# A graph-attention kernel on one core: a half-block opening of its set-up, loads of A tied to their buffers' release, and chunk ends spread over three cycles

## The chip, the cores and the metric

The kernel runs on one core of a Trainium2 chip. A core has TensorE (PE; its weight loads are listed as PEld), VectorE (DVE), ScalarE (ACT), GpSimd (POOL) and SyncE (SP), each with an instruction queue of its own. Transfers are issued from the queues of SP, ACT and POOL. The metric is the device time of one execution in microseconds; the median of several runs counts.

## The reference

Two layers over 4096 nodes with 512 features. The adjacency A (4096 x 4096) holds zeros and ones.

```python
def layer0(X, A, W, a_self, a_neigh, b):           # 8 heads of 64
    feats = einsum('nf,hfo->hno', X, W)
    s_self = einsum('hno,ho->hn', feats, a_self)
    s_neigh = einsum('hno,ho->hn', feats, a_neigh)
    dense = s_self[:, :, None] + s_neigh[:, None, :]
    dense = where(dense > 0, dense, 0.2 * dense) * A[None]
    out = einsum('hij,hjo->hio', softmax(dense, -1), feats) + b[:, None, :]
    return relu(transpose(out, (1, 0, 2)).reshape(N, 512))

x = layernorm(x + layer0(x, adj, ...))
# layer 1: attention inside the graphs that ptr marks (32 of 128 nodes),
# with Wq, Wk, Wv, and scores to which adj is added twice
x = layernorm(x + layer1(x, adj, adj, ptr, ...))
```

## The kernel before

The kernel has a fast path (`adjacency_streamed_path`) and a general path that runs only where the inputs do not have the expected form. Everything below is the fast path. It has a set-up, four passes over A (one for each pair of heads) and layer 1, which is worked into the last passes.

**Order of the work.** TensorE runs its instructions in the order of the program text (`manual_schedule` for PE). On the other engines, and in the three queues that issue transfers, a planner orders the instructions at build time; `keep_in_program_order` pins an instruction to its place in the program. Each queue is worked off in its order: an instruction that waits holds everything behind it.

**Set-up** (the block that begins with the pools `setup1`, `setup2`). The rows of x are worked in eight blocks of four 128-row tiles. `load_rows(k)` fetches block k into `xtp`, which has four buffers, so that a tile of block k+1 can be fetched once the transposes of the same tile of block k are done. Block 0 is issued from SP, all others from ACT. `turn_rows(k)` transposes the sixteen 128x128 pieces of a block into PSUM (L650), and ScalarE copies them, 512 columns at a time, to `xT_f` (L653), adding up `xs` on the way. `features(k, u)` multiplies a tile with W (L722, 8 matmuls, each of which the profile shows as two passes). W has two more columns for each head, the products with a_self and a_neigh, which VectorE works out at the start (L634 and L635); a scored tile reads 264 columns, an unscored one 256. Tiles 0 to 2 of block 0 are not scored there: `first_scores` makes up for them (L746, 12 matmuls of 16 columns). Because of the layout, features 0 and 1 of a block read x tiles 0 and 1 only, and features 2 and 3 read tiles 2 and 3.

VectorE adds b to each result (L733), which also frees its PSUM buffer (`ps_fe`, two of them). `exponentials` works out the softmax factors, and `scaled_features` writes f (`fst`: L775 on ScalarE, L776 on VectorE) and g to DRAM from POOL (L789). For block 0 this comes after `first_scores`. The factors' rows go to `pu_d`.

At the start SP issues x's first block, the two attention vectors, b in two layouts; ACT issues W in four slices and then block 1 of x.

**Passes.** `main_pass(r)` goes through four chunks of 1024 columns of transposed A. In a chunk there are 32 tiles j; with `wide=8` (passes 0 to 2) a chunk is four cycles of eight tiles. In each cycle VectorE makes `q` from p_row, d and the A tile (L1386), ScalarE makes most of the `mark`s from q (L1395), and TensorE does `accf` (A tiles and f, L1406), `acc` (q and g, L1426) and every eight tiles `dens` (marks, L1441). Pass 0 also sums over A (`ae`, L1350), and it makes the A tiles: `load_adjacency` fetches four tiles of A as fp8 from POOL into one of three buffers (L581), `bring` transposes them in pairs (L1130), ScalarE expands them to `at` (L1134), and POOL stores them to `at_d` (L1135) for the later passes. In pass 0, `load_adjacency` is called by `bring` where a group of four tiles is first used; three calls stand in the set-up. f_s, g_s, p_row and u_row come through SP (L1367, L1371, L1331, L1334).

**Chunk ends.** When a chunk is summed, `sums_to_rows` works out `ys` on VectorE (L1180 reads accf and u_row, L1188 adds acc), copies dens (L1190) and, in pass 0, ae (L1195, into the one buffer named hst) on ScalarE, and returns the rest as a generator `pieces`. In pass 0 its steps are: an empty first one; counts n0 and z from ae (L1203 on TensorE, L1208 to L1233 on VectorE); denominators from dens (L1237, L1240 to L1253); the output rows hst (L1260, L1261) and their store hs_d from POOL (L1271). Each `yield` names its price, and `run_pieces(budget)`, called once in a cycle, takes steps until the credit is used up:

```python
state["credit"] += budget
while state["credit"] > 0.0 and (work or ends):
    queue = ends or work
    try:
        state["credit"] -= next(queue[0])
    except StopIteration:
        queue.pop(0)
if not (work or ends):
    state["credit"] = 0.0
```

Before, the budget is 0.75 * wide = 6 in all passes, and a step of pass 0 costs 0.75 * wide = 6, the last one 1.8. So the four steps take one cycle each of the next chunk. In pass 0 the call stands between acc and dens.

Of the kernel before, what the change touches and what calls it, by code (L numbers as in the profile page):

```python
# [19 lines left out]
P = 128  # L20
# [384 lines left out]
def adjacency_streamed_path(  # L405
# [159 lines left out]
    def sums_to_columns(dst, part):  # L565

        for m in range(FC):
            nc.tensor.matmul(
                dst[:, m : m + 1], part[:, ts(m, P)], pick_col, start=True, stop=True
            )  # L570

    ats = {}
    a_bs = {}
# [12 lines left out]
    with tc.tile_pool(name="setup1", bufs=1, side="right") as one, tc.tile_pool(  # L586
# [12 lines left out]

        def load_rows(k):  # L600
            xts[k] = []
            for u in range(4):
                xt = xtp.tile([P, F], F32, name="xt_f")
                queue = nc.scalar if k else nc.sync
                queue.dma_start(xt, x[ts(4 * k + u, P), :])
                xts[k].append(xt)

        load_rows(0)
        FW = FH + 2
        w_sb = one.tile([P, FC, H, FW], F32, name="w_sb_f")  # L610
        for c in range(FC):
            nc.scalar.dma_start(
                w_sb[:, c, :, :FH], W[:, ts(c, P), :].rearrange("h p o -> p h o")
            )
        a_b2 = staged.tile([P, PR, 2, 2, FP], F32R, name="fst").bitcast(F32)
        a_b2 = a_b2[:, :2].rearrange("p r u s n -> p (r u s n)").rearrange(
            "p (k h o) -> p k h o", k=2, h=H
        )
        for k, v in enumerate((a_self, a_neigh)):
            nc.sync.dma_start(  # L620
                a_b2[:, k].rearrange("p h o -> p (h o)"), broadcast_rows(v, P, H * FH)
            )
        b_row = one.tile([P, H * FH], F32, name="b_row")
        nc.sync.dma_start(b_row, broadcast_rows(b, P, H * FH))
        b_col = one.tile([P, PR], F32, name="b_col")
        nc.sync.dma_start(
            b_col,
            bass.AP(tensor=b.tensor, offset=b.offset, ap=[[1, P], [FP, PR]]),
        )
        load_rows(1)  # L630
        for c in range(FC):
            prod = qp.tile([P, C], F32, name="q").rearrange("p (k h o) -> p k h o", k=2, h=H)
            for k in range(2):
                nc.vector.tensor_mul(prod[:, k], w_sb[:, c, :, :FH], a_b2[:, k])  # L634
                nc.vector.tensor_reduce(w_sb[:, c, :, FH + k], prod[:, k], AX.X, OP.add)  # L635
        powers = one.tile([P, 5, H], F32, name="powers")
        for i, v in enumerate((ALPHA, 1.0, ALPHA - 1.0, 1.0 - ALPHA, -ALPHA)):
            nc.vector.memset(powers[:, i, :], v)
        xs = one.tile([P, FC, NB], F32, name="xs")

        def turn_rows(k):
            xT = xTs[k] = two.tile([P, FC, 4, P], F32, name="xT_f")
            pts = {}

            order = [(u, c) for u in range(4) for c in range(FC)]
            for u, c in order if k == 0 else sorted(order, key=lambda x: x[1]):
                if u == 0:
                    last = k == 0 and c == FC - 1
                    pts[c] = misc([P, 4, P]) if last else pss.tile([P, 4, P], F32, name="ps_set")
                nc.tensor.transpose(pts[c][:, u, :], xts[k][u][:, ts(c, P)], ident)  # L650
            for c in range(FC):
                pt = pts[c]
                nc.scalar.activation(  # L653
                    xT[:, c], pt, AF.Identity, accum_out=xs[:, c, k : k + 1]
                )
# [59 lines left out]
        def features(k, u):  # L715
            pf = psf.tile([P, 2, HB], F32, name="ps_fe")
            pf = pf[:, :, : H * FW // 2].rearrange("p q (h w) -> p q h w", w=FW)
            scored = k > 0 or u == 3
            cols = slice(0, FW if scored else FH)
            for c in range(FC):  # L720
                for q in range(2):
                    nc.tensor.matmul(  # L722
                        pf[:, q, :, cols],
                        tile_j(xTs[k][:, c].rearrange("p u n -> p (u n)"), u),
                        w_sb[:, c, 4 * q : 4 * q + 4, cols],
                        start=(c == 0),
                        stop=(c == FC - 1),
                    )
            if u % 2 == 0:
                sums[k, u // 2] = qp.tile([P, C], F32, name="q").rearrange(  # L730
                    "p (u h o) -> p u h o", u=2, h=H
                )
            nc.vector.tensor_add(  # L733
                sums[k, u // 2][:, u % 2].rearrange("p (q h) o -> p q h o", q=2),
                pf[:, :, :, :FH],
                b_row.rearrange("p (q h o) -> p q h o", q=2, h=H // 2),
            )
            if scored:
                exponentials(k, u, pf[:, :, :, FH:])

        def first_scores():

            ps = pss.tile([P, 4, H, 2], F32, name="ps_set")
            for u in range(3):
                for c in range(FC):
# [7 lines left out]
                    )  # L753
            for u in range(3):
                exponentials(0, u, ps[:, u].rearrange("p (q h) w -> p q h w", q=2))

        def scaled_features(k, u):
            j, v, i = 4 * k + u, u // 2, u % 2
            fb = sums[k, v][:, i]
            if i == 0:  # L760
# [14 lines left out]
            nc.scalar.activation(fst[:, :, i, 0, :], fr, AF.Copy, scale=-1.0)  # L775
            nc.vector.scalar_tensor_tensor(  # L776
                fst[:, :, i, 1, :],
# [4 lines left out]
                op1=OP.subtract,  # L782
            )
            if i:
                for dst, n, src in (
# [4 lines left out]

        turn_rows(0)
        for k in range(NB):
            for u in range(4):
                features(k, u)
                if u == (0 if k else 2) and k + 1 < NB:
                    turn_rows(k + 1)
# [4 lines left out]
                if u == 2 and k:  # L801
                    columns_of_exponentials(k - 1)
                if u == 2 and k == 0:
                    first_scores()
# [311 lines left out]
    def bring(r, c, j):  # L1116
# [12 lines left out]
        for t in range(CT):  # L1129
            nc.tensor.transpose(pt[:, t, :], pairs[:, t, :], ident_b)  # L1130
        both = pt.rearrange("p t n -> p (t n)").bitcast(FP8).rearrange("p (n k) -> p n k", k=2)
        for k in range(2):
# [192 lines left out]
    def main_pass(r, ae=None, wide=4):  # L1325

        for c in range(NCH):
            p_row = []
            for h in range(2):
                p_row.append(rowp.tile([P, C], F32, name=f"p_row{h}"))  # L1330
                nc.sync.dma_start(p_row[h], broadcast_rows(pu_d[2 * r + h, ts(c, C)], P, C))  # L1331
            u_row = urowp.tile([P, C], F32, name="u_row")
            for h in range(2):
                nc.sync.dma_start(  # L1334
                    u_row[h * FH : (h + 1) * FH, :],
                    broadcast_rows(pu_d[H + 2 * r + h, ts(c, C)], FH, C),
                )
            def pieces(c, group, place):
                if r == PR - 1 and c:
                    run_plan(PLANS[c == NCH - 1][group][place])  # L1340
                elif place == (r == 0):
                    run_pieces(0.75 * wide)

# [17 lines left out]
            for j0 in range(0, NT, wide):  # L1361
# [3 lines left out]
                for k in range(j0 // 4, (j0 + wide) // 4):  # L1365
                    f_s[k] = fsp.tile([P, 4, 2, FP], F32R, name="f_s")
                    nc.sync.dma_start(  # L1367
                        f_s[k].rearrange("p u s n -> p (u s n)").bitcast(F32), f_d[r, k]
                    )
                    g_s[k] = gfp.tile([P, 4, 2, FH], F32, name="g_s")  # L1370
                    nc.sync.dma_start(g_s[k].rearrange("p u h o -> p (u h o)"), g_d[r, k])  # L1371
                if at_step == 0:
# [178 lines left out]
```

## Time and profile before

| what | value |
|---|---|
| median of 3 runs | 2066.62 us (2066.22 to 2067.95) |
| the profiled execution, its own time | 2068.04 us |
| its span, first to last instruction | 2066.2 us |
| set-up, from the first feature matmul to pass 0 | 13.93 to 165.16 us, TensorE busy 146.68 |
| pass 0 | 165.16 to 592.31 us, TensorE busy 423.32, VectorE 350.15, ScalarE 368.72 |
| passes 1 to 3 with layer 1 | 592.31 to 2066.2 us, TensorE busy 1456.69 of 1473.89 |

The profile is one execution. A row of a timeline gives start and duration in microseconds, the engine, the line of the program, the operation, what it writes and reads, and in brackets how long the engine had been idle and what ended that. ACTq, SPq and POOLq rows are the issues of transfers. In a row of windows each engine has its busy time, then follow the granted TensorE clock (1.00 is full speed), the mean busy share of the transfer engines and GB/s.

### The profile page before, as it was taken

Reading aid. Unit: us, or ns where it says so; the run is one execution under the profiler, and the core shown is the slowest. Engines: PE = TensorE matmul, PEld = TensorE weight load, DVE = VectorE, ACT = ScalarE, POOL = GpSimd, SP = SyncE. Lnnn points to the kernel's source line nnn. Section 1 sums busy time; section 2 is a strip of 40 time slices with the busy share of each in tenths; the row PEclk is TensorE's granted clock in tenths of the full one; section 3 lists DMA queues with packets and bytes.
Section 4 is the critical chain, followed back from the end, with each engine's and each line's share of the span. In section 5 each row is a group of like instructions: output and inputs, shape, how many; then the busy total and the mean of one; then the engine's idle time right before and its main releaser. Section 6 shows DMA issues by size and latency. Waiting matters only on the chain.

```text
span 2066.2 us, 38253 instructions
## 1 busy us (share of the span) xinstructions
PE 2030.9 (98%) x15086; PEld 1049.8 (51%) x15086; DVE 1670.1 (81%) x2125; ACT 1540.4 (75%) x1869; POOL 222.9 (11%) x361
## 2 busy tenths in 40 slices
PE   8999999999999999999999999999999999999997
PEld 6885555444445444444445444444454445445443
DVE  5667888888799998798999899998975884896654
ACT  3338888888878899788899899998885666567420
POOL 1223222222100000000000000000210210210111
PEclk9999999999999999999999999999999999999999
DMA  6989999999899999798999899989974773684211
GB/s 195 303 270 248 270 294 263 296 260 297 264 341 335 367 347 350 258 312 293 327 308 338 300 354 329 329 287 360 315 247 150 240 262 128 229 275 167 74 49 43
DMA packets 207371, 551.31 MB, mean 267 GB/s; under 512 B 24780, under 2 KB 65740, under 8 KB 207180
## 3 DMA queue, kind: packets, MB, share of 16 engines
q1 hardware_dynamic: 136716, 418.45, 58.1%
q0 software_dynamic: 62272, 121.91, 23.1%
q10 hardware_dynamic: 8192, 8.39, 1.2%
q8 instruction: 121, 1.98, 0.4%
q14 instruction: 70, 0.57, 0.1%
HBM read 491.79 MB, written 107.22 MB: 290 GB/s over the span
## 4 chain that ended last, share of the span: by engine, by line
PE 84%; DMA 7%; issue 4%; DVE 2%; ACT 1%; POOL 1%; POOLq 0%; ACTq 0%; DVEq 0%; SPq 0%
PE acc L1426 36%; PE accf L1406 20%; PE ps_m L1067 5%; PE ps_fe L722 5%; PE ps_m L995 5%; DMA at_d<-at 5%; PE dens L1441 5%; PE ps_m L1022 1%; DVE q L1386 1%; PE ps_m L1081 1%; DMA xt_f<-in_x_dram 1%; ACT mark L1395 1%; PE ps_m L975 1%; PE ps_m L1130 1%; PE ps_m L924 1%
## 5 line engine op out<-in xcount | busy, mean ns | idle before, releaser
L1386 DVE SCALAR_TENSOR_TENSOR q<-p_row,d_all,at 128x1024 f32<-128x1024 f32 x1024 | 1241.9, 1277 | 159.9 <-PE acc L1426 129.3
L1395 ACT ACTIVATE mark<-q,nb_all 128x1024 fp8e4<-128x1024 f32 x896 | 995.5, 1145 | 181.4 <-DVE q L1386 165.8
L1426 PE MATMUL acc<-q,g_s 128*32 128x512 f32 x8192 | 904.2, 593 | 1.4 <-DVE q L1386 0.4
L1426 PEld LDWEIGHTS acc<-q,g_s 128*32 128x32 f32 x8192 | 264.3, 110 | 595.3 <-issue 533.6
L1406 PE MATMUL accf<-at,f_s 128*128 128x512 f32 x2048 | 496.7, 398 | 1.9 <-issue 1.8
L1406 PEld LDWEIGHTS accf<-at,f_s 128*128 128x128 f32 x2048 | 380.5, 189 | 111.4 <-issue 28.1
L1151 ACT ACTIVATE ck<-ck,neg_half_f 128x1024 f32<-128x1024 f32 x128 | 146.0, 1141 | 21.7 <-DMA ck<-in_adj_dram 21.7
L1152 ACT ACTIVATE ck<-ck,neg_quarter 128x1024 f32<-128x1024 f32 x128 | 146.4, 1143 | 1.7
L1441 PE MATMUL dens<-mark,e_b 128*6 128x512 fp8e4 x2048 | 125.9, 379 | 0.9 <-ACT mark L1395 0.9
L722 PE MATMUL ps_fe<-w_sb_f,xT_f 128*128 128x264 f32 (+1 forms) x512 | 121.3, 394 | 4.6 <-ACT xT_f L653 4.6
L1134 ACT CAST at<-ps_m 128x1024 fp32r<-128x1024 fp8e4 x128 | 120.1, 1026 | 5.5 <-ACT mark L1395 3.0
L1067 PE MATMUL ps_m<-wvT,x1T 128*128 128x512 f32 x256 | 114.2, 594 | 0.0
L995 PE MATMUL ps_m<-x1T,M_sb 128*128 128x512 f32 x256 | 112.9, 595 | 0.0
L722 PEld LDWEIGHTS ps_fe<-w_sb_f,xT_f 128*128 128x128 f32 x512 | 100.7, 200 | 19.1 <-ACT xT_f L653 5.0
L1271 POOL DMA_DIRECT2D hs_d<-hst x12 | 10.7, 893 | 834.4 <-DVE hst L1261 816.1
L1391 DVE TENSOR_SCALAR mark<-q,d_all 128x1024 fp8e4<-128x1024 f32 x128 | 95.7, 748 | 4.8
L1441 PEld LDWEIGHTS <-e_b 128*6 128x6 bf16 x2048 | 55.8, 86 | 78.5 <-issue 36.2
L1135 POOL DMA_DIRECT2D at_d<-at x128 | 69.0, 539 | 178.0 <-ACT at L1134 107.4
L995 PEld LDWEIGHTS ps_m<-x1T,M_sb 128*128 128x128 f32 x256 | 48.0, 190 | 59.3 <-issue 58.4
L1067 PEld LDWEIGHTS ps_m<-wvT,x1T 128*128 128x128 f32 x256 | 47.6, 190 | 56.4 <-issue 55.1
L1075 DVE TENSOR_TENSOR v_t<-ps_m,bv_row 128x512 f32<-128x512 f32 x32 | 21.7, 683 | 60.5 <-PE ps_m L1067 60.5
L1002 ACT ACTIVATE zT<-ps_m,zb 128x512 f32<-128x512 f32 x32 | 21.8, 680 | 61.1 <-PE ps_m L995 61.1
(185 smaller groups left out, 1084.2 us busy)
## 6 DMA issues: line engine op xcount, KB each, us to landing
at<-at_d SPq DMA_DIRECT2D x384, 512.0 KB, 6.0
f_s<-f_d SPq DMA_DIRECT2D x128, 512.0 KB, 7.5
at_d<-at POOLq DMA_DIRECT2D x128, 512.0 KB, 14.9
ck<-in_adj_dram SPq DMA_DIRECT2D x128, 512.0 KB, 5.4
g_s<-g_d SPq DMA_DIRECT2D x128, 256.0 KB, 5.7
f_d<-fst POOLq DMA_DIRECT2D x16, 1024.0 KB, 7.2
a_b<-in_adj_dram POOLq DMA_DIRECT2D x32, 512.0 KB, 16.3
p_row<-pu_d SPq DMA_DIRECT2D x32, 512.0 KB, 6.7
```

Source lines behind the costliest of these rows:

```text
L722: nc.tensor.matmul(pf[:, q, :, cols], tile_j(xTs[k][:, c].rearrange("p u n -> p (u n)"), u), w_sb[:, c, 4 * q : 4 * q + 4, cols], start=(c ...
L995: nc.tensor.matmul(pz, L1["M"][:, f, ts(c, P)], x1T[:, f, :], start=(f == 0), stop=(f == FC - 1),)
L1067: nc.tensor.matmul(pv, x1T[:, f, ts(u, P)], L1["wvT"][:, f, :], start=(f == 0), stop=(f == FC - 1),)
L1134: nc.scalar.copy(at, both[:, :, k])
L1151: tc.keep_in_program_order(nc.scalar.activation(ck, ck, AF.Square, bias=neg_half))
L1152: nc.scalar.activation(ck, ck, AF.Abs, bias=neg_quarter, accum_out=binp[:, k : k + 1])
L1386: nc.vector.scalar_tensor_tensor(q, p_row[h], d_j, ats[r, c, j].bitcast(F32), op0=OP.max, op1=OP.mult)
L1391: nc.vector.tensor_scalar(mark, q, d_j, None, op0=OP.is_gt, saturate=False)
L1395: nc.scalar.activation(mark, q, AF.Sigmoid, bias=nb_all[:, j, hh : hh + 1], scale=BIG, saturate=False,)
L1406: nc.tensor.matmul(accf[:, s, :], f_s[j // 4][:, j % 4, w, :], ats[r, c, j][:, ts(s, HB)], start=(j == 0 and w == 0), stop=(j == NT - 1 an ...
L1426: nc.tensor.matmul(acc[o : o + 32, s, :], g_s[j // 4][:, j % 4, h, o % FH : o % FH + 32], qs[j, h][:, ts(s, HB)], start=(j == 0), stop=(j ...
L1441: nc.tensor.matmul(dens[lo : lo + 6, :], e_b[:, j, 2 * r + h, :], marks[j, h][:, ts(s, HB)], start=(j == 0), stop=(j == NT - 1),)
```

## The change

Set-up: block 0 of x is worked in two halves. SP now issues all loads of x and half of W, in a new order: x tiles 0 and 1, W slices 2 and 3, the two vectors (in two buffers), x tiles 2 and 3, b, and then the other blocks; ACT issues W slices 0 and 1 only and then runs a one-column activation. TensorE first does transposes of the identity, whose result nobody reads, then tiles 0 and 1; tiles 2 and 3 are transposed in the middle of features(0, 1), into the same PSUM tiles. All four tiles of block 0 are now scored by `first_scores`, and block 1 is transposed after features(0, 3) instead of after features(0, 2). The score columns of W slices 2 and 3 are worked out on VectorE after features(0, 0) and features(0, 1).

Loads of A: in pass 0, right after the transposes that read a buffer for the last time (j % 4 == 2), the load that reuses this buffer is issued, pinned, for the tiles 12 after the buffer's own first one.

Chunk ends: the budget of pass 0 is 1.0 * wide = 8; the prices stay.

Some loads of the first chunks of pass 0 on SP, and one VectorE instruction of block 0, are pinned to the program order.

```diff
+    def in_order(pinned, ins):
+        if pinned:
+            tc.keep_in_program_order(ins)
...
-        def load_rows(k):
-            xts[k] = []
-            for u in range(4):
+        def load_rows(k, us=range(4)):
+            xts.setdefault(k, [])
+            for u in us:
                 xt = xtp.tile([P, F], F32, name="xt_f")
-                queue = nc.scalar if k else nc.sync
-                queue.dma_start(xt, x[ts(4 * k + u, P), :])
+                nc.sync.dma_start(xt, x[ts(4 * k + u, P), :])
                 xts[k].append(xt)
-        load_rows(0)
+        load_rows(0, (0, 1))
...
         for c in range(FC):
-            nc.scalar.dma_start(
+            queue = nc.scalar if c < FC // 2 else nc.sync
+            queue.dma_start(
                 w_sb[:, c, :, :FH], W[:, ts(c, P), :].rearrange("h p o -> p h o")
             )
+        nc.scalar.activation(neg_quarter, neg_quarter, AF.Identity)
...
         for k, v in enumerate((a_self, a_neigh)):
+            nc.sync.dma_start(a_s[k], broadcast_rows(v, P, H * FH))
+        load_rows(0, (2, 3))
         b_row = one.tile([P, H * FH], F32, name="b_row")
         nc.sync.dma_start(b_row, broadcast_rows(b, P, H * FH))
+        load_rows(1)
...
+        def turn_rows(k, us=range(4)):
+            if us[0] == 0:
+                xTs[k] = two.tile([P, FC, 4, P], F32, name="xT_f")
+                turned.clear()
...
+            def keep_warm(n):
+                pw = psf.tile([P, 2, HB], F32, name="ps_fe")
+                for i in range(n):
+                    nc.tensor.transpose(pw[:, 0, :P], ident, ident)
+
+            order = [(u, c) for u in us for c in range(FC)]
             for u, c in order if k == 0 else sorted(order, key=lambda x: x[1]):
+                if (k, c) == (0, 0) and u < 2:
+                    keep_warm((9, 2)[u])
+                nc.tensor.transpose(turned[c][:, u, :], xts[k][u][:, ts(c, P)], ident)
...
-            scored = k > 0 or u == 3
+            scored = k > 0
...
+                if (k, u, c) == (0, 1, 1):
+                    turn_rows(0, (2, 3))
...
-            for u in range(3):
+            for u in range(4):
...
-        turn_rows(0)
+        turn_rows(0, (0, 1))
         for k in range(NB):
             for u in range(4):
                 features(k, u)
-                if u == (0 if k else 2) and k + 1 < NB:
+                if k == 0 and u < 2:
+                    score_columns(FC // 2 + u)
+                if u == (0 if k else 3) and k + 1 < NB:
                     turn_rows(k + 1)
...
-                if u == 2 and k == 0:
+                if u == 3 and k == 0:
                     first_scores()
...
         for t in range(CT):
             nc.tensor.transpose(pt[:, t, :], pairs[:, t, :], ident_b)
+        ahead = c * NT + j + 10
+        if j % 4 == 2 and ahead < NCH * NT :
+            tc.keep_in_program_order(load_adjacency(ahead // NT, ahead % NT))
...
                 elif place == (r == 0):
-                    run_pieces(0.75 * wide)
+                    run_pieces((0.75 if r else 1.0) * wide)
```

Where the diff is cut, it has the pins of SP's loads (p_row and u_row of the first two chunks of pass 0, f_s and g_s of its first two cycles), `score_columns`, which holds the former loop body of the score products, and the narrower evacuation in `turn_rows`, which sums block 0's second half into a ninth column of `xs`.

## The prediction

> **What bounds the kernel now.** I read the page's engine rows first, then the waits of TensorE in the first 640 us, then the engines' timelines where those waits lie. Row 1 of the page says that TensorE is the bound: 2030.9 of 2066.2 us. So only TensorE's idle time, a slower TensorE clock, or TensorE work that appears or goes can move the time; a wait on another engine counts where TensorE runs into it.
>
> ```profile
> PE 2030.9 (98%) x15086; PEld 1049.8 (51%) x15086; DVE 1670.1 (81%) x2125; ACT 1540.4 (75%) x1869; POOL 222.9 (11%) x361
> ```
>
> TensorE's waits up to 640 us (total, times, longest):
>
> ```profile
> PE ps_set L650 <- DMA xt_f<-in_x_dram: 6.4, 4, 3.9
> PE ps_fe L722 <- ACT xT_f L653: 4.6, 1, 4.6
> PE ps_m L1130 <- ACT at L1134: 2.0, 2, 1.2
> PE accf L1406 <- issue: 1.8, 1, 1.8
> PE ps_set L695 <- ACT pu_j L671: 1.3, 1, 1.3
> PE ps_m L1130 <- DVE hst L1214: 1.0, 3, 0.4
> PE dens L1441 <- ACT mark L1395: 0.9, 2, 0.7
> ```
>
> These seven are all in that stretch. A wait on loads of A (a_b) is not among them.
>
> The opening, on ScalarE, TensorE and TensorE again:
>
> ```profile
> 7.39 4.47 ACTq L605 DMA_DIRECT2D xt_f<-in_x_dram  x4
> 11.89 1.28 ACT L653 ACT_TABLE_LOAD   x1 [11.89 <-DMA w_sb_f<-in_L_gnn_W_dram]
> 13.19 0.60 ACT L653 ACTIVATE xT_f<-ps_set 128x512 f32<-128x512 f32 x1
> ...
> 13.93 12.03 PE L722 MATMUL ps_fe<-w_sb_f,xT_f 128*128 128x256 f32 x48 [4.61 <-ACT xT_f L653]
> ...
> 92.68 1.76 PE L650 MATMUL ps_set<-ident_f,xt_f 128*128 128x128 f32 x13 [1.24 <-DMA xt_f<-in_x_dram]
> ```
>
> ScalarE stands in its own DMA issues until 11.89 (the second block of x waits there for its buffers), then loads its table, and only then evacuates transposes that were complete at 9.3. Features start at 13.93. Block 5's x is late once more, at 92.
>
> The chunk ends, in the first pass's windows (one 8-tile cycle each; span, then busy PE, PEld, DVE, ACT) and timelines:
>
> ```profile
> 271.13:296.92 25.79, 25.79 (x245) 13.14 (x242) 21.77 (x20) 23.18 (x25) 6.07 (x10) 1.00 1.12 278
> 377.38:404.41 27.03, 26.37 (x244) 13.08 (x242) 24.23 (x22) 21.59 (x23) 6.09 (x10) 1.00 1.11 296
> ...
> 387.62 0.59 ACT L1195 COPY hst<-ae 128x512 f32<-128x512 f32 x1 [4.41 <-DMA hs_d<-hst]
> ...
> 590.93 1.27 DVE L1180 SCALAR_TENSOR_TENSOR ys<-accf,S_col,u_row 128x1024 f32<-128x1024 f32 x1
> ...
> 592.31 7.59 PE L1406 MATMUL accf<-at,f_s 128*128 128x512 f32 x32 [1.76 <-issue]
> ```
>
> Both windows are the first cycle of a chunk. In the first, no earlier result occupies hst; in the second, ScalarE's copy of ae waits 4.4 us for the store of the hst written one cycle before, marks come late, and TensorE pays. The last two lines are the step from pass 0 to 1: accf is released only when VectorE has done ys, behind two hst products of 1.28 us together; the row names "issue", but TensorE starts 0.1 us after ys ends.
>
> **The opening.** It removes ScalarE's x issues and half of its W issues, and loads its table early (issues to about 1.8, table 1.28: ready near 3.3). The first two tiles of x landed 3.0 and 4.5 us after issues at 0.73 and 1.15, so at 3.7 and 5.65; they stay first on SP. Four transposes took 1.1 us, so x1's end at 6.75, with the half-width evacuations beside them (half of 0.6 plus 0.2 each). W's second slice landed at 7.5 (issue 1.2, 6.3 us); its first precedes it. I take 6.8 for the first feature matmul, bounds 6.3 and 8.
>
> From there on TensorE: 264-column passes run 3.73 us for 16, 0.233 each, so 256 columns 0.226. Tiles 0 to 3 are 64 passes (14.5 us), the second eight transposes 1.0, the next sixteen 2.0, first_scores 32 passes at 3.13/24 = 0.13 (4.2), features(1,0) 3.7. Sum 25.4: block 2's transposes at 32.2 if the clock were full. Against before this order holds 16 score columns' matmuls instead of 12 (+1.0) and brings the second half's transposes onto the path (+1.0).
>
> The clock is not full. The granted clock shows no record before 17, but the first transposes took 421 ns and later ones 273, so the opening was slow: 12.03 us against 48 x 0.226 = 10.85. The one-microsecond windows show 0.50 from 30.7 to 34.1, after first_scores, and there 32 passes took 8.91 instead of 7.46. I charge the new start 1.6, and first_scores, longer now and with transposes just before it, 1.5 to 3.0. Transposes of block 2 then start at 35.3 to 36.8, before at 39.47: **3.4 us gained**, bounds 1 and 6.
>
> The change also adds eleven transposes of the identity, before x arrives and while x1 is awaited (9 x 0.27 = 2.4 us from 1.4: no delay). The Trainium skill, TensorE: Matmul & The Clock Gate, Part 4, speaks against them: transposes do not count as activity for the clock. The rows agree as far as they go (8 transposes between 7.3 and 9.3 raised nothing), but never show eleven in a row. By the rule the 1.6 stay; without it they go. Yet the third tile can't profit: its transposed rows wait on ScalarE behind fst, which needs VectorE's first add. That add follows four score products and four reductions (0.65 each) and a 0.22 cast from a_self's landing, which I put at 9.0 to 9.6 (now 9.0): add at 14.9 to 15.6, fst 0.63, evacuation 0.4, so 16.6. TensorE gets there at 16.7 by the slow sum. So a fast clock is worth at most some tenths here, and I take the rule.
>
> W's last slices move to SP and x's second half behind the vectors. The skill's Trainium Kernel Development and Optimization, Key Constraints, says that queues share the same DMA engines and only issue time is saved: by it I count no earlier bytes from two queues, only ScalarE's 11.89. The trace moved 262 GB/s over the first 13.93 us; ten transfers of 256 KB ahead of b_row put x2 and x3 at about 11, needed at 13.8.
>
> **Loads of x on SP.** They are issued as TensorE frees each buffer, with ScalarE's evacuations and issue gaps no longer between (block 5: transposes end 75.9, issues 76.5 to 77.9, landing up to 14.7). The early loads of f_s, g_s, p_row and u_row now stand behind them; they are needed at 160 and follow near 110. Block 5's delay goes: its transposes to features took 3.33 (90.95 to 94.28) against 1.87 elsewhere, **1.5 us**. Bounds 0 and 1.5. Block 2's x is the nearest to a new wait: issues 25 to 26.5, 5.3 us landing as at 29, needed at 35: 3 us spare.
>
> **Loads of A.** Now pinned on POOL right behind the transposes that free a buffer. TensorE waits for none before, and POOL waited for TensorE 23 times before such a load, so most already leave at the release; the first ones leave 4 to 15 us sooner. Worth 0. If it were harmful: at 0.85 to 1.05 DMA share after 163 these loads delay f_s of the second cycle, issued 171.5 to 175.5, needed 193.75, usually 7.5 in flight: 10 us of cover.
>
> **Chunk ends.** The budget per cycle rises from 6 to 8 while the price of a piece stays 6, so the empty first yield and the n0 piece both fall in the first cycle, the dens piece in the second, the output in the third. The same TensorE instructions: chunk 1's four windows are 25.79, 27.03, 26.50, 26.93, of which 25.8 is the plain cycle. What goes is what chunks 2 and 3 have above chunk 1: 27.03 + 27.42 + 26.49 + 26.94 = 107.88 against 106.25, and 26.19 + 27.39 + 26.53 = 80.11 against 79.32: **2.4 us**, since hs_d (10.5 us to land) now has a whole cycle before ae is copied. The short n0 wait (0.33 each, three times) moves and stays. At the pass step the hst products have gone a cycle earlier, and the changed program's order on VectorE puts ys ahead of the last eight q of the chunk: the 1.76 become about 0.2: **1.6 us**. Bounds of both: 1.5 and 4.2. VectorE has 3.9 us per cycle to spare, and n0's reductions are 2.1.
>
> **Sum:** 3.4 + 1.5 + 0 + 2.4 + 1.6 = 8.9. Behind the first cycles of pass 1 the instruction order is the old one and TensorE 99% busy, so it carries through. The profiled run took 2068.0 for a span of 2066.2; its sum gives a span of 2057.3 and 2059.1 outside. It lay 1.4 above the median of the runs, so the median becomes 2066.6 - 8.9 = **2057.7**.
>
> **Rivals.**
> *The opening gives almost nothing.* Two more slow windows of 3.4 us cost 1.7 each, or W or a_self lands 3 us late. For it: first_scores has already throttled the clock once; before pass 0 it was 0.50 for 10 us. Against: matmul stretches on both sides. Then 8.9 - 3.4 = 5.5: 2061.
> *More.* The clock windows fall well (their phase against the work is not fixed) and pass 0's slow start, 9.99 us for 32 accf passes that later take 7.6, loses less: 8.9 + 3 to 4: 2054.
> *Moved waits.* The opening gives 1 and n0 in the first cycle meets the late marks, keeping the 2.4: 1.5 + 1.6 + 1 = 4.1: 2062.5, within what can be told from nothing.
> *Slower: u_row holds SP at the pass step.* The changed order puts pass 1's u_row ahead of f_s on SP; it waits for ys, which releases the old one. If ys ran at 590.9 as now, f_s would leave at 592.2 instead of 575.9 and land 7.5 later; TensorE, ready at 590.5, would start near 602 instead of 592.3: 9.7 lost, 7.3 gained elsewhere, 2069. It decides once ys ends later than about 582. Against: ys only needs accf, complete at 572.9.
>
> **Numbers.** The forecast's case has 0.56, opening lost 0.20, more 0.12, moved waits 0.08, slower 0.04. A measurement here tells about 0.2%, 4.1 us, from no change. The forecast, "more" and most of the lost opening (0.17) are beyond that: faster 0.85, the same 0.11, slower 0.04. The range 2053.5 to 2063 reaches from "more" to the lost opening.
>
> **What would show it.** First feature matmul at 6.3 to 8; block 2's transposes at 35 to 37; no wait on xt_f after that; first cycles of chunks 2 and 3 alike at about 27; no 4 us wait before ae's copy; accf of pass 1 within 0.3 us of the last dens. I am wrong if SP holds u_row for ys, if the clock shows 0.50 in more windows, or if the second half of block 0 makes TensorE wait.

## The result and the profile after

The changed kernel takes **2056.78 us** (median of 6 runs, 2054.87 to 2059.1), the kernel before, run beside it, 2067.21 (6 runs, 2064.97 to 2070.18): ratio 0.9949, 95% interval 0.9936 to 0.9962, or 10.4 us less. The profiled run took 2055.59, with a span of 2053.8; the one before had 2066.2. Where these 12.4 us of span lie, by the start times of TensorE's instructions:

| stretch | before | after | difference |
|---|---|---|---|
| start to block 2's transposes (opening) | 39.47 | 33.65 | -5.8 |
| from there to pass 0's first accf | 125.69 | 124.11 | -1.6 |
| pass 0 | 427.15 | 423.56 | -3.6 |
| passes 1 and 2 | 772.29 | 772.42 | +0.1 |
| pass 3 and the rest | 701.6 | 700.1 | -1.5 |

The last row is not put down to the change: it is all in pass 3's seventh cycle (12.36 to 10.86), which lasted from 10.85 to 13.23 us in the thirteen profiles of this study with no relation to what was edited; its cause was not looked for.

TensorE's line of busy times in the page of the changed kernel, and its waits up to 640 us:

```profile
PE 2028.2 (99%) x15105; PEld 1051.6 (51%) x15105; DVE 1671.7 (81%) x2125; ACT 1540.6 (75%) x1878; POOL 226.6 (11%) x361
```

```profile
PE ps_m L1165 <- ACT at L1172: 2.4, 2, 1.6
PE accf L1454 <- DMA f_s<-f_d: 1.5, 1, 1.5
PE ps_fe L671 <- POOL ident_f masks.py:199: 1.4, 1, 1.4
PE ps_set L725 <- ACT pu_j L701: 1.3, 1, 1.3
PE ps_m L1165 <- DVE hst L1252: 1.0, 3, 0.4
PE ps_set L677 <- DMA xt_f<-in_x_dram: 0.5, 2, 0.3
PE ps_fe L752 <- ACT xT_f L680: 0.2, 1, 0.2
```

The 6.4 us for x and the 4.6 us for xT_f have shrunk to 0.5 and 0.2, and no dens waits for marks. New is the second row: accf waits 1.5 us for an f_s.

The opening on TensorE, in the changed kernel's timeline (start, length, line, what, count):

```profile
6.72 7.68 PE L752 MATMUL ps_fe<-w_sb_f,xT_f 128*128 128x256 f32 x24
...
17.23 7.18 PE L752 MATMUL ps_fe<-w_sb_f,xT_f 128*128 128x256 f32 x32 [0.22 <-ACT xT_f L680]
24.25 2.03 PE L677 MATMUL ps_set<-ident_f,xt_f 128*128 128x128 f32 x16
26.21 3.94 PE L778 MATMUL ps_set<-w_sb_f,xT_f 128*128 128x16 f32 x32
30.00 3.81 PE L752 MATMUL ps_fe<-w_sb_f,xT_f 128*128 128x264 f32 x16
33.65 2.09 PE L677 MATMUL ps_set<-ident_f,xt_f 128*128 128x128 f32 x16
```

Features start at 6.72 instead of 13.93, and the second half-block is met with a wait of only 0.22. The sixteen features after first_scores take 3.81: that is full speed. In the profile before, the granted clock was 0.50 at that place.

The same first cycles of chunks 1 and 2 as were shown of before, now in the changed kernel's windows (span; busy PE, PEld, DVE, ACT, POOL; granted clock; DMA share; GB/s), and below them the step into pass 1 in the timelines of SP, VectorE and TensorE, by time:

```profile
262.74:289.75 27.01, 26.67 (x248) 13.37 (x245) 22.99 (x28) 23.69 (x25) 6.67 (x10) 1.00 1.12 286
369.03:396.16 27.13, 26.78 (x248) 13.39 (x245) 23.39 (x28) 23.96 (x26) 6.18 (x10) 1.00 1.11 292
```

```profile
554.84 13.44 SPq L1155 DMA_DIRECT2D at<-at_d  x8
563.41 1.28 DVE L1218 SCALAR_TENSOR_TENSOR ys<-accf,S_col,u_row 128x1024 f32<-128x1024 f32 x1 [2.15 <-PE accf L1454]
568.38 1.09 SPq L1377 DMA_DIRECT2D u_row<-pu_d  x2
569.52 0.92 SPq L1411 DMA_DIRECT2D f_s<-f_d  x1
581.32 7.59 PE L1454 MATMUL accf<-at,f_s 128*128 128x512 f32 x32 [1.46 <-DMA f_s<-f_d]
```

Chunks 1 and 2 are alike, and ScalarE's copy of ae waits for no store. The first cycle of chunk 1 is 1.2 us longer, since it now holds a piece; the fourth cycles are 1.1 shorter. ys runs at 563.4, long before it is needed (before, it ran at 590.9, at the last moment). But f_s, which SP has put behind eight loads of at and two of u_row, is now the last to arrive.

### The profile page after: what moved, and what is told of

It is laid out like the page before. It is cut to its first block, busy times and chain, and to the rows that moved or that the text cites. A ratio compares the mean times of both kernels' runs of the same rounds, so it can differ in the third digit from the quotient of the medians.

```text
span 2053.8 us, 38310 instructions
## 1 busy us (share of the span) xinstructions
PE 2028.2 (99%) x15105; PEld 1051.6 (51%) x15105; DVE 1671.7 (81%) x2125; ACT 1540.6 (75%) x1878; POOL 226.6 (11%) x361
## 4 chain that ended last, share of the span: by engine, by line
PE 92%; DVE 4%; DMA 1%; issue 1%; SPq 0%; POOL 0%; ACT 0%; POOLq 0%; DVEq 0%
PE acc L1474 40%; PE accf L1454 23%; PE ps_m L1102 5%; PE ps_fe L752 5%; PE dens L1489 5%; PE ps_m L1030 5%; DVE q L1434 3%; PE ps_m L1165 1%; PE ps_m L1057 1%; PE ps_m L1116 1%; PE ps_m L1010 1%; PE ps_m L959 1%; PE ps_set L677 1%; PE ps_m L1298 1%; PE ae L1394 1%
```

## The experiments

All times are medians beside runs of the kernel before on the same chip, in three batches in which it took 2067.38, 2066.67 and 2067.31. A difference between two changed kernels goes across batches; by the intervals it is known to some 3 us. The change has three parts, and six kernels cover every combination of them beside the kernel before and the changed one (last row):

| set-up (opening, x on SP) | early chunk ends | rule for loads of A | us | before | ratio (95%) | difference by the ratio |
|---|---|---|---|---|---|---|
| new | - | - | 2065.87 | 2067.38 | 0.9994 (0.9985 to 1.0002) | -1.2 |
| - | new | - | 2064.24 | 2067.38 | 0.9985 (0.9978 to 0.9991) | -3.1 |
| - | - | new | 2077.20 | 2067.38 | 1.0040 (1.0027 to 1.0054) | +8.3 |
| new | new | - | 2062.46 | 2066.67 | 0.9979 (0.9971 to 0.9986) | -4.3 |
| - | new | new | 2064.00 | 2067.31 | 0.9984 (0.9977 to 0.9991) | -3.3 |
| new | - | new | 2073.86 | 2067.31 | 1.0034 (1.0024 to 1.0044) | +7.0 |
| new | new | new | 2056.78 | 2067.21 | 0.9949 (0.9936 to 0.9962) | -10.5 |

The single parts add up to +4.0; together they give -10.5. The rest of this section shows what lies between.

### One part alone: the set-up

```diff
-        ahead = c * NT + j + 10
-        if j % 4 == 2 and ahead < NCH * NT :
-            tc.keep_in_program_order(load_adjacency(ahead // NT, ahead % NT))
...
-                    run_pieces((0.75 if r else 1.0) * wide)
+                    run_pieces(0.75 * wide)
```

(from the changed kernel)

> The kernel before with the set-up of the changed kernel alone (half-block opening, x loads on SP, pinned order); loads of A and chunk ends as before. Theory (the set-up's gain reaches the end undiminished): in the changed kernel's trace the opening was 5.8 us and the rest of the set-up 1.6 us shorter, so the time is 7 to 8.5 us below before (ratio about 0.996), pass 0 starts at 157 to 159 us, and its cycles keep before's values of 27.0 and 26.2 in the chunk ends' third and fourth place. Rival A (the gain is partly the clock): the clock falls to 0.50 after the first scores as it did before, block 2's transposes start at 35 to 37 us, and the gain is 4 to 6 us. Rival B (pass 0 waits for its loads of A after all without the new rule): L1165's transposes or the at copies wait in the first cycles of pass 0, and 2 us or more of the set-up's gain are gone there.

The theory missed: -1.2 us, which the interval does not tell from nothing. What both rivals named is in the trace. The clock is at 0.50 for 6.8 us after first_scores (block 2's transposes at 37.3, a little past rival A's 35 to 37), pass 0 starts at 161.8 and is 430.98 long, 3.8 longer than before's. Its first cycle lasts 30.58 instead of 28.59, for TensorE waits 2.57 us for a load of A, and chunk 2's first cycle lasts 29.72 instead of 27.03: the copy of ae waits 7.1 us there for hs_d instead of 4.4.

### One part alone: the chunk ends

```diff
-                    run_pieces(0.75 * wide)
+                    run_pieces((0.75 if r else 1.0) * wide)
```

(from the kernel before)

> The kernel before with one number changed: pass 0's budget for chunk-end pieces is 1.0 x wide. Theory (what the changed kernel's trace shows): the two cycles that hold the late pieces get 1.5 and 0.8 us shorter in sum over chunks 1 to 3, and the step into pass 1 gains no more than 0.3 us, because the first f_s is now issued behind 8 loads of at and two of u_row: 2.6 us below before in all, ratio 0.9987. By the prediction's own sum 4.0 us (0.9981), with a wait of 0.2 us at the step. Rival (u_row's loads hold SP more where pass 0 starts later): the wait at the step is as long as before's 1.8 or longer and the gain 2 us or less.

Measured: -3.1 us (-4.5 to -1.9), which fits the theory's 2.6 and the prediction's own 4.0. In its profile pass 0 lasts 422.96, 4.2 less than before's, as in the prediction's sum. At the step there is no wait in this profile: f_s is issued 12.4 us after the last cycle's first accf, and accf of pass 1 starts 24.1 after it.

### One part alone: the rule for the loads of A

```diff
             nc.tensor.transpose(pt[:, t, :], pairs[:, t, :], ident_b)
+        ahead = c * NT + j + 10
+        if j % 4 == 2 and ahead < NCH * NT :
+            tc.keep_in_program_order(load_adjacency(ahead // NT, ahead % NT))
```

(from the kernel before)

> The kernel before with only the new rule for the loads of A in pass 0 (issued at the release of their buffer, pinned). Theory: worth nothing, -0.5 to +0.5 us, since no instruction of TensorE waited for a load of A before. Rival (the loads now run beside other transfers that are on the path, or they hold POOL's queue ahead of the at_d stores): 1 to 3 us slower, with at_d's median landing above 16 us and a longer wait of the at copies. Rival (an unseen wait on A was in pass 0): 1 us or more faster, in the first cycles of pass 0.

Measured: +8.3 us, more than the first rival's bound, and not where it was looked for: at_d's median landing is 14.4 us (before 14.9), and the copies to at wait 4.5 us for their transposes in all of pass 0 instead of 2.5. The timeline of ScalarE in this kernel, and the windows of its chunk 2's first cycle and of 8 us in that cycle:

```profile
391.85 0.58 ACT L1198 COPY hst<-ae 128x512 f32<-128x512 f32 x1 [8.93 <-DMA hs_d<-hst]
```

```profile
377.08:410.39 33.31, 30.34 (x244) 14.51 (x242) 27.54 (x24) 23.34 (x24) 6.09 (x10) 0.90 1.11 279
...
402.00:404.00 2.00, 0.76 (x4) 0.17 (x4) 2.00 (x3) 2.00 (x3) 0.00 (x0) 1.00 1.10 247
404.00:406.00 2.00, 1.11 (x4) 0.17 (x4) 2.00 (x3) 2.00 (x3) 0.00 (x0) 0.51 1.16 209
406.00:408.00 2.00, 1.55 (x19) 0.59 (x19) 2.00 (x2) 2.00 (x3) 0.00 (x0) 0.50 1.24 111
408.00:410.00 2.00, 2.00 (x20) 1.25 (x13) 2.00 (x3) 2.00 (x3) 0.00 (x0) 0.50 1.14 264
```

hs_d's store is issued at 376.0, as before (376.3), but lands 15.8 us later instead of 11.3. The copy of ae holds ScalarE for 8.9 us instead of 4.4; marks come late, TensorE is busy for 0.76 of 2 us, and then its clock is halved for the work that is there again. The cycle lasts 33.31 instead of 27.03, chunk 3's 31.32 instead of 26.19.

### Is that wait the whole loss? A buffer of its own for the copy of ae

```diff
-            aes = hp_.tile([P, CT, FP], F32, name="hst")
-            aes = aes.rearrange("p t n -> p (t n)")[:, :HB]
+            aes = more["aes"].tile([P, HB], F32, name="aes")
...
-        main_pass(0, ae, wide=8)
+        with tc.tile_pool(name="aesp", bufs=1) as more["aes"]:
+            main_pass(0, ae, wide=8)
```

(from the kernel before with the rule for the loads of A)

> The kernel before with the rule for the loads of A, and the copy of ae put into a buffer of its own, so that it waits for no store of hs_d. Theory (that wait is the whole loss of the rule): the first cycles of chunks 2 and 3 last 26 to 27 us instead of 33.3 and 31.3, no half clock there, pass 0 is 424 to 426 us long, and the time is 1 to 3 us below before, 9 to 11 below the rule alone. Rival (the loss has another cause, and the wait is only where it shows): the first cycles stay at 29 us or more and the time is 4 us or more above before.

Measured: 2064.22 us beside 2067.31, ratio 0.9985 (0.9978 to 0.9991), -3.1 us: 11 below the rule alone. Windows of its chunks 2 and 3, first cycles:

```profile
377.19:403.00 25.81, 25.81 (x244) 13.14 (x241) 23.02 (x21) 22.65 (x23) 6.11 (x10) 1.00 1.10 297
483.48:509.27 25.79, 25.79 (x244) 13.10 (x241) 23.03 (x21) 22.62 (x23) 6.07 (x10) 1.00 1.10 301
```

TensorE is busy throughout, though chunk 1's hs_d lands as late here as with the rule alone (15.6 us after its issue): nothing waits for it any more. So the rule's loss is that one buffer, shared by two uses. Why the store lands later was not separated: the loads of A and the store both go through POOL's queue, and the DMA share is 1.0 to 1.2 either way. The rule is not the only thing that delays it, for with the new set-up alone, without the rule, the same store took 14.0 us.

### The rule together with each other part

The kernel before with early chunk ends and the rule, and the changed kernel with the late ends (budget 0.75 again):

> The kernel before with the early chunk ends and the rule for the loads of A. Theory (with early ends the rule has nothing to hold up): no wait of the copy of ae, pass 0 423 us long as with early ends alone, 2.5 to 4 us below before. Rival (the rule costs by itself, by fuller transfer engines): pass 0 longer than 425, 0 to 2 us below before or slower.

> The changed kernel with the chunk ends given out as before (budget 0.75), so set-up and loads of A alone. Theory (the rule for the loads of A lengthens the store of hs_d, on which the copy of ae waits only while the chunk ends are late): the copy waits 7 to 9 us in chunks 2 and 3, these chunks' first cycles last 30 us or more, TensorE's clock falls there in one or both, and the time is 6 to 11 us above the changed kernel, 4 below to 1 above before. Rival (the rule's loss in the run with it alone came from the late opening, whose first cycles it disturbed): first cycles of chunks 2 and 3 of 27 us, and 2.5 to 4 us above the changed kernel.

With early ends the rule is harmless: pass 0 422.67 us, -3.3 in all, no wait of the copy on hs_d. With late ends it costs as much on the new set-up as on the old: first cycles of 34.60 and 31.56 us, in which the copy waits 10.2 and 7.8 us (the theory had 7 to 9). Its time was set too low: 17 us above the changed kernel instead of 6 to 11, for these two cycles alone are 7.5 and 4.6 longer than the changed kernel's.

### Is the rule needed at all? The changed kernel without it

The three lines of the rule are taken out of the changed kernel.

> The changed kernel without its rule for the loads of A (they are issued again where the scheduler puts them). Theory (the rule is needed by the early opening): as with the set-up alone, three loads of A are issued in one bunch behind at_d stores at about 178, L1165's transposes wait some 2.6 us for a_b at about 191, marks come late, and pass 0 is 3 to 5 us longer than the changed kernel's 423.6: 3 to 5 us above the changed kernel, 5.5 to 7.5 below before. Rival (the rule is worth nothing, as the prediction had it, once the chunk ends are early): within 1 us of the changed kernel, 9.5 to 11.5 below before. Rival (the rule costs in the changed kernel too, as it did alone): 1 us or more below the changed kernel.

The theory holds, at somewhat more than its 3 to 5 us: 2062.46, 5.7 above the changed kernel, and no run of either reaches the other's range (2060.63 to 2069.32 beside 2054.87 to 2059.1). Its timelines of POOL and TensorE:

```profile
176.37 0.53 POOL L1170 DMA_DIRECT2D at_d<-at  x1 [0.38 <-ACT at L1169]
176.90 2.67 POOL L586 DMA_DIRECT2D a_b<-in_adj_dram  x3
...
191.02 1.07 PE L1165 MATMUL ps_m<-ident_b,a_b 128*128 128x128 bf16 x16 [3.20 <-DMA a_b<-in_adj_dram]
```

The planner puts three loads of A in one bunch behind four at_d stores. In the kernel before it had put them at 171.3, 182.2 and 186.5, in the changed kernel the rule has them at 155.9, 160.3 and 175.2. The first two cycles last 30.98 and 27.38 us, in the changed kernel 27.54 and 25.79, and pass 0 is 4.0 longer. In the second cycle TensorE is busy throughout, but its granted clock is 0.50 from about 192.1 to 195.7: the wait is paid for a second time in clock.

### x on ScalarE again

```diff
-                nc.sync.dma_start(xt, x[ts(4 * k + u, P), :])
+                queue = nc.scalar if k else nc.sync
+                queue.dma_start(xt, x[ts(4 * k + u, P), :])
```

(from the changed kernel)

> The changed kernel with the loads of x from block 1 on issued by ScalarE again. Theory (the prediction's 1.5 us for loads of x on SP, block 5's late x): the set-up from block 2's transposes to pass 0 takes 125.7 us again instead of 124.1, with a wait of 1.2 us for xt_f near block 5, and, since block 1's x is issued on ScalarE behind W's and the dummy activation, no delay in the opening: 1.6 us above the changed kernel. Rival (ScalarE's issues of block 1 and 2 stand in front of the opening's evacuations): the first feature matmul is 3 us or more later than 6.7, and the time 4 to 7 us above. Rival (nothing): within 0.5 us.

Measured: 2062.01 beside 2066.67, ratio 0.9972 (0.9962 to 0.9983): 5.2 above the changed kernel, which is the first rival, with part of the theory's loss. The nine runs spread widely: three lie between 2056.93 and 2057.87, in the changed kernel's range, the others above 2060.7. ScalarE's timeline:

```profile
8.13 1.52 ACTq L610 DMA_DIRECT2D xt_f<-in_x_dram  x2
9.70 0.38 ACT L681 ACTIVATE xT_f<-ps_set 128x256 f32<-128x256 f32 x1 [6.35 <-DMA w_sb_f<-in_L_gnn_W_dram]
```

Two loads of block 1 stand in ScalarE's queue ahead of the evacuations, which could have begun at 6.2. They do not wait for their buffers, which TensorE had left by 6.4. In the trace each is held by the completion semaphore of an earlier transfer, which it uses again: the loads leave at 8.13 and 9.30, right after W's slices 2 and 3 have landed (8.03 and 9.20). That is why the row names W. Features start at 10.2 instead of 6.7, and the rest of the set-up takes 125.14 instead of 124.11.

### No transposes of the identity

```diff
-                if (k, c) == (0, 0) and u < 2:
-                    keep_warm((9, 2)[u])
```

(from the changed kernel)

> The changed kernel without its eleven transposes of the identity. By the rule that transposes do not wake the clock: the first 24 feature passes take 7.7 us as in the changed kernel (full speed from about 11.4), block 2's transposes start within 0.3 us of the changed kernel's where the clock after the first scores is the same, and the time is the same to 0.5 us. Rival (they do wake it earlier): the first 24 passes take 8.5 us or more, full speed comes 1.5 us or more later, and the time is 1 to 1.6 us longer.

Measured: 2057.93, ratio 0.9956 (0.9944 to 0.9969). The interval overlaps the changed kernel's (0.9936 to 0.9962), so the time tells neither from the other. The first 24 feature passes, from TensorE's timeline:

```profile
6.72 7.09 PE L750 MATMUL ps_fe<-w_sb_f,xT_f 128*128 128x256 f32 x24
```

With the eleven transposes they took 7.68 in the changed kernel's profile. In this pair they brought full speed no earlier, which is what the Trainium skill, TensorE: Matmul & The Clock Gate, Part 4, would have (transposes do not count as activity). Two other kernels contradict it as a rule. With x on ScalarE, TensorE had run nothing but transposes when they became shorter:

```profile
4.59 0.35 PE L678 MATMUL ps_m<-ident_f,xt_f 128*128 128x128 f32 x1
4.77 0.38 PE L672 MATMUL ps_fe<-ident_f 128*128 128x128 f32 x2
5.75 0.55 PE L678 MATMUL ps_set<-ident_f,xt_f 128*128 128x128 f32 x3 [0.59 <-DMA xt_f<-in_x_dram]
```

and in the changed kernel they had not:

```profile
5.68 0.90 PE L677 MATMUL ps_set<-ident_f,xt_f 128*128 128x128 f32 x3 [0.35 <-DMA xt_f<-in_x_dram]
```

One transpose alone takes 0.27 us there instead of 0.42. In the kernel with the late ends (new set-up and rule) the same happens at about 5.5. In the other five kernels with the transposes of the identity, and in all six without them, every transpose ahead of the first feature matmul kept the slow length. So transposes alone can be followed by full speed; two of seven against none of six does not show that the eleven are what brings it. It gains nothing here: with the late ends the 24 passes took 5.50 us, but TensorE then waited 1.51 us for xT_f, and the second half's features started at 17.30, in the changed kernel at 17.23.

### The step into pass 1: u_row behind f_s, and f_s ahead of four at loads

```diff
+            late_u = r > 0 and c == 0
+            if not late_u:
                 for h in range(2):
...
                         u_row[h * FH : (h + 1) * FH, :],
...
                     g_s[k] = gfp.tile([P, 4, 2, FH], F32, name="g_s")
...
+                if late_u and j0 == 0:
+                    for h in range(2):
...
+                                u_row[h * FH : (h + 1) * FH, :],
```

(from the changed kernel)

> The changed kernel, and at the start of passes 1 to 3 the two loads of u_row are issued behind the first cycle's f_s and g_s instead of ahead of them. Theory (f_s is late at the step into pass 1 because of SP's order, u_row being the piece of it that the change put there): the first f_s is issued 1.1 us earlier and lands without 512 KB of u_row beside it, so the wait of the first feature matmul of pass 1, 1.46 us, falls to 0.5 or less: 1.0 to 1.5 us below the changed kernel, about 11.5 us below before. Rival (the loads of at are what f_s stands behind and shares the transfer engines with): the wait stays at 1.0 us or more and the time is within 0.5 us of the changed kernel's 10.4 us below before.

```diff
                 for x_ in follow[:first]:
                     bring(*x_)
+                if r == 0 and (c, j0 + wide) == (NCH - 1, NT):
+                    for k in range(wide // 4):
+                        early_f[1, 0, k] = load_f(1, 0, k)
```

(in addition to the first; `load_f` holds the former load of f_s, and the pass takes what lies in `early_f` instead of loading again)

> The changed kernel with u_row's loads behind f_s and g_s as before, and pass 1's first two f_s issued in pass 0's last cycle already, ahead of the last four loads of at. Theory (the last thing at the step is f_s, held by loads of at that wait for their buffers): the first f_s is issued when its buffer comes free, some 8 us earlier than with u_row moved alone, the step has no wait for f_s and the cycle across it lasts 24.0 as it did with u_row moved alone: 1.5 us below the changed kernel and no better than with u_row alone. Rival (the 23.99 us of that run still hold a wait): below 23.8. Rival (the two f_s hold back the four loads of at): waits for at in pass 1's first cycle, above 23.2 in it.

SP and TensorE in the first of these kernels:

```profile
556.58 13.06 SPq L1155 DMA_DIRECT2D at<-at_d  x8
569.69 0.48 SPq L1413 DMA_DIRECT2D f_s<-f_d  x1
...
581.53 3.72 PE L1465 MATMUL accf<-at,f_s 128*128 128x512 f32 x15
```

f_s leaves 12.2 us after the last cycle's first accf (557.54) instead of 13.7, and the wait is gone: the last cycle lasts 23.99 us in both kernels, 25.52 in the changed one. u_row ahead costs f_s more than its 1.1 us of issue: f_s also lands 11.7 us after it is issued, and 8.9 with u_row behind it. So the place is shown. The second kernel issues f_s 8 us earlier still and gains no more, so 24.0 is what the cycle takes without a wait. The first cycle of pass 1 lasts 23.13 us there, so the loads of at are not held back either. In the time it can't be seen: 2056.66 (ratio 0.9950, 0.9936 to 0.9963) and 2056.89 (0.9949, 0.9936 to 0.9962) beside the changed kernel's 2056.78. An interval of 5 us does not resolve 1.5, and the profiles show the 1.5 to be above the average: with u_row ahead of f_s the wait was 1.46, 1.2, 1.2, 0.7, 0.5 and 0 in six kernels. Neither version is shown to beat the changed kernel.

### The clock after first_scores

No kernel was made for this; the thirteen profiles of this study bear on it. The granted clock after first_scores was 0.50 for no, one or two stretches of 3.4 us:

| set-up | kernels (profiled run) | stretches at 0.50 | block 2's transposes start |
|---|---|---|---|
| new | changed kernel; f_s ahead | 0 | 33.6, 33.7 |
| new | u_row behind; no identity transposes | 1 | 35.2, 35.5 |
| new | rule out; late ends; set-up alone | 2 | 36.8, 37.0, 37.3 |
| old | ae's own buffer | 0 | 38.9 |
| old | before; early ends; ends and rule; rule alone | 1 | 39.5, 39.3, 39.4, 40.2 |

(x on ScalarE, 40.0 with two, is left out of it.) A stretch costs 1.6 to 1.7 us, by how much longer first_scores and the features behind it take. With two of them, in the changed kernel without the rule, TensorE's rows read:

```profile
26.11 5.07 PE L778 MATMUL ps_set<-w_sb_f,xT_f 128*128 128x16 f32 x32
31.02 5.95 PE L752 MATMUL ps_fe<-w_sb_f,xT_f 128*128 128x264 f32 x16
36.80 2.09 PE L677 MATMUL ps_set<-ident_f,xt_f 128*128 128x128 f32 x16
```

against 3.94 and 3.81 in the changed kernel's profile: the same instructions, with nothing waited for in either.

## Why the prediction was right, point by point

It said 2057.7 (2053.5 to 2063.0) and the median is 2056.78: 8.9 us of gain expected, 10.4 measured, an interval of 7.9 to 13.2.

The number owes something to luck. The prediction gave the rule for the loads of A nothing, so its 8.9 was also its forecast for the changed kernel without that rule. That kernel measured 4.3 (2.9 to 6.0) below before, 4.6 less than the forecast, because the new set-up brought a wait for A that the sum did not have. The rule, put at 0, is worth 5.7 there and filled the gap.

- **Opening, 3.4 us (bounds 1 to 6): right as an average.** 6.8 for the first feature matmul was 6.72. x tiles 2 and 3 landed at 12.4 and 13.1, not about 11, still ahead of their transposes at 14.25. The second half's features started at 17.23 where the sum had 16.7, with a wait of 0.22. The profiled run gained 5.8, because the term for first_scores' clock, 1.5 to 3.0 us, did not fall due in it. Over seven profiles with the new set-up (without x on ScalarE) block 2's transposes start at 35.6 on average (the prediction had 35.3 to 36.8), over the five with the old one at 39.5: 3.9 us.
- **Three readings behind the opening were wrong and did no harm.** ScalarE's x loads did not wait for buffers alone: the third left at 11.04, right after W's third slice had landed (10.97), though TensorE had left its buffer at 8.46. The slow stretch put at 30.7 to 34.1 lasted from about 30.4 to 33.9, the same 3.4 us. And transposes are not without effect on the clock, as two kernels show; what held was the other argument, that a fast clock gains at most tenths before the second half's features.
- **Loads of x on SP, 1.5 us: right for what it named** (set-up after the opening 125.69 to 124.11), but it is also a condition of the opening: with x on ScalarE the opening loses 3.5 us as well. The prediction had the reason (ScalarE stands in its own issues) and counted it under the opening, which is where it belongs.
- **Loads of A, 0: the step that failed, though the sum did not show it.** Inside the whole change the rule is worth 5.7 us; alone it costs 8.3. The prediction argued that no TensorE instruction waits for A in the profile before. That was so with the planner's order for the old program; for the new set-up it bunches three loads, and 3.2 us of wait appear. Which part of the set-up makes it do so was not separated. And the rule moves what POOL's queue carries: with late chunk ends the store of hs_d lands 15.8 us after its issue, and the copy of ae, already waiting 4.4, waits 8.9. The changed kernel has the remedy for both: the rule undoes the bunching, and the early ends free the buffer.
- **Chunk ends, 2.4 us: right, and for the reason given** (the store has a whole cycle, and the copy of ae waits for nothing). In the changed kernel's trace chunk 2 is 1.5 us shorter, and chunk 3, up to the step, 0.8: 2.3.
- **Pass step, 1.6 us: the mis-sized term.** It took ys for the only thing late and left 0.2 us of wait; of its 1.6 us 0.3 came in the profiled run. ys did come early, but the wait became one for f_s, 1.46 us in the profiled run, 0 to 1.5 in the others with u_row ahead (mean 0.8). This is the rival "u_row holds SP" in a mild form: u_row did not wait for ys (564.7, far from the 582 at which that decides), but its two issues take 1.1 us ahead of f_s, which then lands later too.
- **Not foreseen:** 1.0 us in pass 0's first cycles. The granted clock was 0.50 for three stretches around the pass's start in the profile before and for two in the one after, the prediction's rival "more" in a small form. It is not put down to the change: the first cycle took 27.2 to 28.6 us in the four other kernels with the old set-up.

## What to carry to other kernels

Parts of a change that share a queue or a buffer do not add: a load moved to its buffer's release can cost 8 us or be worth 6, depending on whether a store behind it holds a buffer that another engine needs. When an opening is changed under a planner, look at what the planner does next with the order of the queues; a wait that is absent from the profile before can be absent because of the old order. A load that leaves late need not wait for its buffer: look for the earlier transfer whose landing comes just before. And when the last wait at a place is removed, list everything due there with its own time of arrival (here ys, then f_s) before counting the gap as gained.

## What the runs showed of the hardware that was not expected

The granted clock fell while TensorE was busy without a gap. In the changed kernel without the rule, windows around first_scores (columns as above):

```profile
27.00:28.00 1.00, 1.00 (x10) 1.00 (x11) 0.00 (x0) 0.73 (x3) 0.00 (x0) 1.00 0.78 250
28.00:35.00 7.00, 7.00 (x27) 6.18 (x27) 3.79 (x14) 1.46 (x12) 0.90 (x1) 0.54 0.32 113
```

TensorE is busy for 7.00 of 7 us (the profile models the ends of matmuls) and is granted 0.54. What precedes are sixteen transposes (2.0 us) and 32 passes of 16 columns (3.9 us at full speed). That the stretches are 3.4 us long and fall differently from run to run agrees with the free-running window of 3.41 us that the Trainium skill, TensorE: Matmul & The Clock Gate, Part 1, describes; that a stretch of narrow matmuls counts as idle is what these rows suggest. It was not tested by widening them, and the transposes ahead of them may have a part in it.
